# A graph layer on one core: W's first products in the chain from keys and values to the mix, and other places for the quads around it

## The chip, the cores and the metric

The kernel runs on one core of one Trainium2 chip. The metric is the device time of one execution in microseconds (us), lower is better. The core's engines each run their own instruction stream in order: PE (matrix products; PEld is its weight load), DVE (vector), ACT (scalar and activation), POOL (here it issues the row gathers and computes small powers), and SP (issues plain DMA transfers). They wait for each other through semaphores.

## The reference

The input is x, 12500 rows of 256 float32, and 200,000 edges sorted by destination. The layer adds three terms to x:

```python
xn = _layernorm(x)
support = xn @ W_gnn
agg = segment_sum(support[src] * edge_weight[:, None], dst, N)      # relu(agg) is added to x
k, v = layernorm per head of xn @ wk.T, xn @ wv.T                   # 4 heads of 64, with gains and biases
kv = einsum('bhsd,bhse->bhde', k, v) / S
mix = (q @ kv) @ wo.T + bo,  q = xn @ wq.T                          # added to x
x = x + ffn(_layernorm(x))
# ffn, 30 times: h += 0.01 tanh(h); h = silu(h); h = layernorm(h) * w + b; h = h @ W + bias
```

Since q, kv and wo act on xn one after the other, the whole attention term is xn times one 256 x 256 matrix. The kernel calls this matrix `mix`; it exists only when kv has been summed over all rows. Since W_gnn is linear, the kernel sums gathered rows of xn first and multiplies the sums by W afterwards.

## The kernel before

**Units.** Rows come in 98 tiles of 128; four tiles make a group (25 groups). Edges come in 1563 columns of 128. A gather (L182, an indirect DMA that POOL issues) fetches the 128 source rows of one column from xnd in DRAM. Four columns are a *quad* (391 of them), two quads an *octet*. `selections` builds on DVE the 0/1 and weight matrices of a quad (L208, L213) and, with the second quad, of its octet (L221). `sum_quad` (L234) multiplies four gathered tiles into the PSUM tile pq; `copy_quads` (L245, ACT) copies pq of a finished octet to sq; `add_quads` (L259) spreads it over 192 destination rows in the PSUM ring pa; `free_nodes` copies finished columns of pa to aT (L273, ACT) and clears them (L274, DVE). aT of a group is complete when its last octet is added; then W can be applied.

**Gathers.** Gather buffers are a ring of 16 (`ROWS`): a gather is issued only while `gathered < summed * 4 + 16`, so each `sum_quad` is followed by `gathers(4)`.

**Stages.** (1) Load and normalize x, write xnd, transpose xn into xnT, and the first 24 key tiles. (2) From tile 24 on, the loop at L793: per tile `KeyValue` (L288: xn times the key and value weights; L295 and L301 on ACT, L299, L305, L306 on DVE normalize it) and `kv_product` of the tile two before (L314, into pacc). A list `quad_at` says after which tiles a quad is summed; the quads' selections stand between the tile's two DVE halves. Also, small weight preparations (`rest`), whose inputs SP loads at the beginning of this stage. (3) The chain from keys and values to the mix: psum_kv (L823) is pacc copied; py (L828) = psum_kv times the key gains; y (L831) its copy; pbd (L835) = y times the value gains; bd (L838) its diagonal blocks; a product with wq (L846); `at` (L848 to L851) its centred copy; a product with wo (L855); mix (L860). Between its links stand five calls of `another_quad`. (4) The passes. `plan()` writes the order out beforehand with fixed costs: in each step one item, either "mix" of a group (L1009: xn times mix, then x is added, L1076), or "W" of a group (L1009: aT times W, L1080 adds a correction accw, L1081 applies relu and adds), or a "pass" of the 30 (transposes L996, product L1009, then ACT and DVE), and beside it quads, gathers and the start of a group. A group starts after its mix and W. At most five groups are in flight. An item's loads and transposes are issued in step k, its product in k + 1, what follows in k + 2. `accw` holds zeros, or another matrix of sums where a rare branch (L622) was taken; the register n_out chooses.

**Buffers.** The chain's PSUM tiles come from p_kv, three in rotation; the products of stage 4 from p_o, two in rotation; the loads of x and accw in stage 4 from two tiles xt, which reuse SBUF of the stages before, so that the first waits until the mix is done.

Of the kernel before, what the change touches and what calls it, by code (L numbers as in the profile page):

```python
# [8 lines left out]
F32 = mybir.dt.float32  # L9
# [7 lines left out]
P = 128  # L17
# [13 lines left out]
def gps_layer(  # L31
# [135 lines left out]
    class Edges:  # L167
# [2 lines left out]
        summed = 0  # L170
        added = 0
        freed = 0
        xg, sel, selq, sq, aT = {}, {}, {}, {}, {}
        pq = None

# [64 lines left out]
    def copy_quads():  # L240
        if ed.pq is not None and (ed.summed % 2 == 0 or ed.summed == NQ):
            o = (ed.summed - 1) // 2
            rows = min(Q, NE - o * O) * 2 * WIN
            sq = ge.tile([P, C], F32, name="sq")
            nc.scalar.copy(sq[:rows], ed.pq[:rows])  # L245
            ed.pq = None
            ed.sq[o] = (rows, sq)
# [18 lines left out]
    def free_nodes():  # L266
        while ed.freed < NS and last_of[ed.freed] < ed.added:
            j = ed.freed
            gi = j * SLOT // (G * P)
            if gi not in ed.aT:  # L270
                ed.aT[gi] = ge.tile([P, KC, G * P], F32, name="aT", bufs=3)
            c, d = (j % RING) * SLOT, j * SLOT % (G * P)
            nc.scalar.copy(ed.aT[gi][:, :, d : d + SLOT], pa[:, :, c : c + SLOT])  # L273
            nc.vector.memset(pa[:, :, c : c + SLOT], 0.0)  # L274
            ed.freed += 1
# [437 lines left out]
    with ExitStack() as ph:  # L713
# [14 lines left out]
        lk = w1.tile([D + 1, P // D, P], F32, name="lk")  # L728
        rv = w1.tile([D + 1, D], F32, name="rv")
        gcol = w1.tile([D, 2], F32, name="gcol")  # L730
        wo_nat = w1.tile([P, KC, C], F32, name="wo_nat")
        nc.sync.dma_start(out=wo_nat, in_=wo.rearrange("(k p) c -> p k c", p=P))
        f_nat = w1.tile([P, KC, C], F32, name="f_nat")
# [51 lines left out]

        quad_at, spent, n = {}, 0.0, 0
        for t in range(kv_done, NT + 2):
            quad_at[t] = spent > 7.0 + 5.2 * n
            n += quad_at[t]
            spent += 2.5 + (1.1 if quad_at[t] else 0.0)  # L790
        gathers(ROWS)
# [18 lines left out]
                sum_quad()  # L810
                gathers(Q)

        def another_quad():
            copy_quads()
            free_nodes()
            selections(1)
            add_quads()
            sum_quad()
            gathers(Q)


        psum_kv = w1.tile([D + 1, HEADS, D + 1], F32, name="psum_kv")
        nc.vector.tensor_copy(psum_kv, pacc)  # L823
        bd = w1.tile([P, KC, P], F32, name="bd")
        nc.vector.memset(bd, 0.0)
        py = p_kv.tile([D + 1, HEADS, P], F32, name="pkv")
        for hd in range(HEADS):
            nc.tensor.matmul(py[:, hd, :], lhsT=psum_kv[:, hd, :], rhs=lk[:, hd % (P // D), :], start=True, stop=True)  # L828
        another_quad()
        y = w1.tile([D + 1, HEADS, P], F32, name="y")  # L830
        nc.vector.tensor_copy(y, py)  # L831
        another_quad()
        pbd = p_kv.tile([P, HEADS, D], F32, name="pkv")
        for hd in range(HEADS):
            nc.tensor.matmul(pbd[:, hd, :], lhsT=y[:, hd, :], rhs=rv, start=True, stop=True)  # L835
        for hd in range(HEADS):
            r = slice(hd % (P // D) * D, (hd % (P // D) + 1) * D)
            nc.vector.tensor_scalar(bd[r, hd // (P // D), r], pbd[r, hd, :], 1.0 / N, None, ALU.mult)  # L838
        another_quad()


        at = w1.tile([P, KC, C], F32, name="at")
# [1 line left out]
        pm = p_kv.tile([P, KC, C], F32, name="pkv")  # L844
        for h in range(KC):
            nc.tensor.matmul(pm[:, h, :], lhsT=bd[:, h, :], rhs=wq_n[:, h, :], start=True, stop=True)  # L846
        another_quad()
        nc.vector.tensor_copy(at, pm)  # L848
        nc.vector.tensor_reduce(am, at, AX.X, ALU.add)
        nc.vector.tensor_scalar(am, am, 1.0 / C, None, ALU.mult)  # L850
        nc.vector.tensor_tensor(at, at, am[:, :, None].to_broadcast([P, KC, C]), ALU.subtract)  # L851
        pm = p_kv.tile([P, KC, C], F32, name="pkv")
        for m in range(KC):
            for h in range(KC):
# [1 line left out]
                    pm[:, m, :], lhsT=at[:, h, m * P : (m + 1) * P], rhs=woT[:, h, :],  # L856
                    start=(h == 0), stop=(h == KC - 1),
                )
        another_quad()
        nc.vector.scalar_tensor_tensor(  # L860
            mix, bo_r[:, None, :].to_broadcast([P, KC, C]), 1.0 / C, pm, op0=ALU.mult, op1=ALU.add
        )
# [8 lines left out]
    def plan():  # L871
        T_PASS, T_MATRIX, T_QUAD, T_GATHER, T_LAND, T_POW, T_STATS, T_CHAIN = 4.4, 3.5, 1.2, 1.25, 6.0, 1.3, 4.4, 14.0
        now, pool = 0.0, 4.0
        quads, got, started = ed.summed, ed.gathered, []
        whole, based = [], {}
        active, mixed, steps, k = {}, 0, [], 0
        landed = {t: 0.0 for t in range(got)}
        summed, passes = 0, 0
        pows = {}
        while len(based) < len(groups) or active or len(started) < len(groups):  # L880
            item, nq, cost, start = None, 0, 0.0, None
            octets = NO if quads == NQ else quads // 2
            while summed < len(groups) and octets > last_of[min((summed + 1) * G, NT) * P // SLOT - 1]:
                whole.append(summed)
                summed += 1
            ready = [g for g, (last, it, at) in active.items() if last + APART <= k and at <= now + 1.0]

            wanted = whole and mixed <= whole[0]
            if wanted or (not whole and not ready and mixed < len(groups)):
                item, cost = ("mix", mixed), T_MATRIX  # L890
                mixed += 1
            elif whole:
                item, cost = ("W", whole.pop(0)), T_MATRIX
                based[item[1]] = k
            elif ready:

                lead = 0 if len(started) == len(groups) else 1
                g = min(
                    ready, key=lambda g: (
                        active[g][1] + FFN_ITERS * (g // ABREAST) + lead * (g % ABREAST), active[g][0]  # L900
                    ),
                )
                it = active[g][1]
                passes += 1
                item, cost = ("pass", g, it), T_PASS
                if it == FFN_ITERS - 1:
                    del active[g]
                else:
                    active[g] = (k, it + 1, now + T_CHAIN)
                    pows[k + 2] = pows.get(k + 2, 0) + 1  # L910
            if (
                len(active) < ABREAST and len(started) in based and based[len(started)] + 3 <= k
                and (not started or k >= started[-1] + 4)
            ):
                start = len(started)
                started.append(k)
                active[start] = (k + 3, 0, now + 26.0)
                pows[k + 1] = pows.get(k + 1, 0) + 1
                pows[k + 5] = pows.get(k + 5, 0) + 1

            ng, pool = 0, max(pool, now)
            while got < min(NE, quads * Q + ROWS) and pool < now + (T_STATS - T_GATHER if pows.get(k) else max(cost, 1.0)):
                pool += T_GATHER
                landed[got] = pool + T_LAND
                got += 1
                ng += 1
            if pows.get(k):
                pool = max(pool, now + T_STATS) + T_POW * pows[k]
            ahead = 2 * G * P / STEP * (ABREAST + 0.2 + passes / FFN_ITERS)
            while quads < min(NQ, ahead) and nq < (1 if item else 2):  # L930
                if max(landed.get(t, 1e9) for t in range(quads * Q, min(NE, (quads + 1) * Q))) > now + cost:
                    break
                quads += 1
                nq += 1
                cost += T_QUAD
            steps.append((item, nq, start, ng))
            now += max(cost, 1.0)
            k += 1
        return steps
# [82 lines left out]
    for k in range(K + 3):  # L1022
# [40 lines left out]
        if kind2 == "pass" and not last:  # L1063
            act2(g2, pos.pop((kind2, g2)), s2)
        elif last:
            t0, nt = groups[g2]
            for q in range(nt // 2):
                h = pos[kind2, g2][:, q].rearrange("p c j -> p j c")
                r = slice(2 * q, 2 * q + 2)
                nc.vector.tensor_tensor(base[g2][:, r, :], h, base[g2][:, r, :], ALU.add)  # L1070
            pos.pop((kind2, g2))
            rows_io(out, base[g2], t0, nt, False, nc.sync)
            written[g2] = k
        elif kind2 == "mix":
            nt = groups[g2][1]
            nc.vector.tensor_tensor(base[g2], pos.pop((kind2, g2))[:, :nt, :], xts.pop((kind2, g2))[:, :nt, :], ALU.add)  # L1076
        elif kind2 == "W":
            nt = groups[g2][1]
            ac = xts.pop((kind2, g2))[:, :nt, :]
            nc.vector.tensor_tensor(ac, pos.pop((kind2, g2))[:, :nt, :], ac, ALU.add)  # L1080
            nc.vector.scalar_tensor_tensor(base[g2], ac, 0.0, base[g2], op0=ALU.max, op1=ALU.add)  # L1081
# [93 lines left out]
```

## Time and profile before

| | |
|---|---|
| median of 3 runs | 4166.28 us (4165.76 to 4167.11) |
| the profiled execution, its own time | 4167.84 us |
| its span, first to last instruction | 4166.0 us |
| gathers, L182 | 1563, 1594.1 us busy, 1020 ns each |
| products of the passes, L1009 po<-w,zT | 2668.0 us, 380 ns a record |
| quads, L234 | 264.6 us, 392 ns a record |
| key tiles, L288 | 196.5 us, 625 ns a record |
| mean TensorE clock granted | 0.997 |
| first matmul of py (L828), first mix product (L1009) | at 353.31, at 384.47 us |

Every float32 matmul leaves two records, so a quad has eight, a group's product sixteen. Busy times count from a record's start to its modelled end; a matmul that follows another overlaps it. In a timeline a row gives start, length, engine, line, what it writes from what, and in brackets the engine's idle time before it with what ended it. In a row of windows the busy time of PE, PEld, DVE, ACT and POOL follows the stretch and its length, each with the number of instructions, then the granted TensorE clock, the share of the DMA engines and GB/s.

### The profile page before, as it was taken

Reading aid. Unit: us, or ns where it says so; the run is one execution under the profiler, and the core shown is the slowest. Engines: PE = TensorE matmul, PEld = TensorE weight load, DVE = VectorE, ACT = ScalarE, POOL = GpSimd, SP = SyncE. Lnnn points to the kernel's source line nnn. Section 1 sums busy time; section 2 is a strip of 40 time slices with the busy share of each in tenths; the row PEclk is TensorE's granted clock in tenths of the full one; section 3 lists DMA queues with packets and bytes.
Section 4 is the critical chain, followed back from the end, with each engine's and each line's share of the span. In section 5 each row is a group of like instructions: output and inputs, shape, how many; then the busy total and the mean of one; then the engine's idle time right before and its main releaser. Section 6 shows DMA issues by size and latency. Waiting matters only on the chain.

```text
span 4166.0 us, 67989 instructions
## 1 busy us (share of the span) xinstructions
PE 4095.5 (98%) x24201; PEld 3346.7 (80%) x24201; DVE 3397.5 (82%) x7389; ACT 2544.1 (61%) x3762; POOL 2588.0 (62%) x3186
## 2 busy tenths in 40 slices
PE   8998999999999999999999999999999999999999
PEld 5555788888887888888788888888888888788888
DVE  8664788888888888888888888888888888888887
ACT  7431466666666666666666666656666666677776
POOL 3677777777776666666667667667667652222222
PEclk9999999999999999999999999999999999999999
DMA  8434422222222221112221221122222210000000
GB/s 258 120 106 138 142 80 65 77 75 72 71 83 73 60 63 56 56 56 60 89 65 57 67 63 59 54 75 77 66 64 58 65 44 14 16 1 1 1 1 23
DMA packets 147686, 278.35 MB, mean 67 GB/s; under 512 B 28047, under 2 KB 97197, under 8 KB 147341
## 3 DMA queue, kind: packets, MB, share of 16 engines
q0 software_dynamic: 75024, 204.97, 16.9%
q1 hardware_dynamic: 72173, 68.42, 5.3%
q8 instruction: 197, 3.23, 0.3%
q14 instruction: 148, 1.21, 0.1%
q10 hardware_dynamic: 144, 0.52, 0.0%
HBM read 247.68 MB, written 26.12 MB: 66 GB/s over the span
## 4 chain that ended last, share of the span: by engine, by line
PE 81%; DVE 10%; ACT 2%; issue 1%; POOL 1%; DMA 1%; POOLq 0%; ACTq 0%; DVEq 0%
PE po L1009 55%; PE pt L996 14%; PE pq L234 5%; DVE z L982 3%; PE pkv L288 3%; PE pa L259 3%; DVE st L968 2%; DVE s L961 2%; ACT s L955 2%; DMA xg<-xnd,src_i 1%; PE pacc L314 1%; POOL rs L974 1%; DVE f_st L1131 1%; DVE big L1070 0%; ACT s L962 0%
## 5 line engine op out<-in xcount | busy, mean ns | idle before, releaser
L1009 PE MATMUL po<-w,zT 128*128 128x256 f32 x11760 | 2668.0, 380 | 2.5 <-DVE big L1070 1.9
L1009 PEld LDWEIGHTS po<-w,zT 128*128 128x128 f32 x11760 | 2177.9, 190 | 279.6 <-issue 9.5
L182 POOL DMA_INDIRECT xg<-xnd,src_i x1563 | 1594.1, 1020 | 486.5 <-issue 333.3
L961 DVE SCALAR_TENSOR_TENSOR s<-s,po 128x1024 f32<-128x1024 f32 (+1 forms) x725 | 866.6, 1195 | 399.7 <-ACT s L955 398.6
L982 DVE TENSOR_SCALAR z<-s,st,rs 128x256 f32<-128x256 f32 x2940 | 1051.5, 420 | 77.7 <-POOL rs L974 73.8
L962 ACT ACTIVATE s<-s 128x1024 f32<-128x1024 f32 (+1 forms) x750 | 780.5, 1041 | 381.7 <-DVE s L961 376.0
L968 DVE BATCH_NORM_STATS2 st<-s 128x6 f32<-128x512 f32 x1470 | 937.0, 678 | 85.3 <-ACT s L962 85.3
L955 ACT ACTIVATE s<-po 128x1024 f32<-128x1024 f32 (+1 forms) x725 | 731.0, 1008 | 337.9 <-PE po L1009 337.6
L1003 ACT ACTIVATE zT<-pt 128x512 f32<-128x512 f32 x1470 | 800.6, 601 | 97.2 <-PE pt L996 96.4
L996 PEld LDWEIGHTS pt<-ident,z 128*128 128x128 f32 x5880 | 660.4, 142 | 195.6 <-issue 124.1
L996 PE MATMUL pt<-ident,z 128*128 128x128 f32 x5880 | 793.0, 276 | 20.9 <-DVE z L982 20.3
L974 POOL TENSOR_TENSOR rs<-ve,mhalf 128x4 f32<-128x4 f32 (+1 forms) x750 | 773.1, 1031 | 62.4
L972 POOL TENSOR_SCALAR ve<-st 128x4 f32<-128x4 f32 (+1 forms) x750 | 152.7, 204 | 939.6 <-DVE st L968 909.4
L234 PE MATMUL pq<-xg,sel 128*32 128x256 f32 x3126 | 264.6, 392 | 13.8 <-DMA xg<-xnd,src_i 13.8
L245 ACT COPY sq<-pq 128x256 f32<-128x256 f32 x196 | 72.3, 369 | 302.4 <-PE pq L234 302.3
L288 PE MATMUL pkv<-wkv,big 128*128 128x512 f32 x392 | 196.5, 625 | 7.1 <-DVEq L622 5.0
L259 PE MATMUL pa<-selq,sq 128*128 128x192 f32 (+2 forms) x1168 | 181.5, 291 | 1.0 <-ACT sq L245 1.0
L234 PEld LDWEIGHTS pq<-xg,sel 128*32 128x32 f32 x3126 | 65.4, 108 | 140.7 <-issue 114.5
L259 PEld LDWEIGHTS pa<-selq,sq 128*128 128x128 f32 x1168 | 169.5, 191 | 10.9 <-ACT sq L245 2.0
L273 ACT COPY aT<-pa 128x128 f32<-128x128 f32 x196 | 51.4, 262 | 203.7 <-PE pa L259 202.2
L288 PEld LDWEIGHTS pkv<-wkv,big 128*128 128x128 f32 x392 | 68.7, 195 | 73.7 <-issue 68.1
L295 ACT ACTIVATE sq<-pkv 128x512 f32<-128x512 f32 x98 | 58.2, 593 | 102.5 <-PE pkv L288 102.5
(150 smaller groups left out, 1523.8 us busy)
## 6 DMA issues: line engine op xcount, KB each, us to landing
xg<-xnd,src_i POOLq DMA_INDIRECT x1563
xt<-in_x_dram SPq DMA_DIRECT2D x48, 512.0 KB
xnd<-xt SPq DMA_DIRECT2D x24, 512.0 KB
xt<-accw SPq DMA_DIRECT2D x24, 512.0 KB
out_dram<-big SPq DMA_DIRECT2D x24, 512.0 KB
xg<-in_dst_dram SPq DMA_DIRECT2D x6, 128.0 KB
xg<-in_src_dram SPq DMA_DIRECT2D x6, 128.0 KB
xg<-in_edge_weight_dram SPq DMA_DIRECT2D x6, 128.0 KB
```

Of the source, the lines that this page charges most:

```text
L182: nc.gpsimd.indirect_dma_start(out=ed.xg[t], out_offset=None, in_=xnd, in_offset=bass.IndirectOffsetOnAxis(ap=src_i[:, t : t + 1], axis=0),)
L234: nc.tensor.matmul(ed.pq[j * 2 * WIN : (j + 1) * 2 * WIN, :], lhsT=sel[:, j, :], rhs=ed.xg.pop(q * Q + j), start=(q % 2 == 0), stop=last, ...
L259: nc.tensor.matmul(pa[:, k, c : c + hi - lo], lhsT=sq[:rows, k * P : (k + 1) * P], rhs=selq[:rows, lo - n0 : hi - n0], start=False, stop=( ...
L955: nc.scalar.activation(flat(s, nt), flat(h, nt), AF.Tanh)
L961: nc.vector.scalar_tensor_tensor(sf, sf, 0.01, flat(h, nt), op0=ALU.mult, op1=ALU.add)
L962: nc.scalar.activation(sf, sf, AF.Silu)
L968: nc.vector.bn_stats(st[:, q, :], s[:, q].rearrange("p c j -> p (c j)"))
L974: nc.gpsimd.tensor_tensor(rs[:, :nt], ve[:, :nt], mhalf[:, :nt], ALU.pow)
L982: nc.vector.tensor_scalar(z[:, j, :], s[:, j // 2, :, j % 2], sv[:, j, 1:2], rs[:, j : j + 1], ALU.subtract, ALU.mult)
L996: nc.tensor.transpose(pt[:, i, k, :], z[:, 2 * q + i, k * P : (k + 1) * P], ident)
L1003: nc.scalar.activation(zT[:, 2 * q : 2 * q + 2], pt, AF.Copy, bias=1.0)
L1009: nc.tensor.matmul(po[:, j // 2, :, j % 2] if paired else po[:, j, :], lhsT=lhsT(j, k), rhs=rhs[:, k, :], start=(k == 0 and (j % 2 == 0 or ...
```

## The change

Six edits act together.

- `quad_at`: no quad after the last nine key tiles (89 to 97); two quads come at their end (with tile 97 where the count so far is even, and at the step after). 40 quads are summed in the loop instead of 45.
- `another_quad` and its five calls go. Two quads are summed (`two_quads`) ahead of py and two ahead of mix, all with their selections built beforehand; at the start of stage 4, 44 quads are summed instead of 50.
- W's product of the first two groups is computed in the chain, two tiles at a time (`w_product`), and stored with accw added over aT itself (`w_stored`).
- The accw rows of these two groups are loaded at the beginning of stage 2 into two new tiles, ahead of wo_nat.
- The planner takes the mixes of these two groups first and gives them no "W" step; a group counts as based with its mix.
- The mix step of these groups applies relu to aT and adds it, in two halves (SCALAR_TENSOR_TENSOR on DVE).

The planner computes the rest of the order anew from 44 quads.

```diff
+        acs = [w1.tile([P, G, C], F32, name=f"ac{g}") for g in range(2)]
+        for g, (t0, nt) in enumerate(groups[:2]):
+            rows = accw[bass.ds(n_out * ((G + t0) * P), nt * P), :]
+            nc.sync.dma_start(out=acs[g], in_=rows.rearrange("(g p) c -> p g c", p=P))
         wo_nat = w1.tile([P, KC, C], F32, name="wo_nat")
...
-            quad_at[t] = spent > 7.0 + 5.2 * n
+            quad_at[t] = t == NT or (t == NT - 1 and n % 2 == 0) or (t < NT - 9 and spent > 7.0 + 5.2 * n)
...
-        def another_quad():
-            copy_quads()
-            free_nodes()
-            selections(1)
-            add_quads()
-            sum_quad()
-            gathers(Q)
+        def two_quads():
+            for _ in range(2):
+                sum_quad()
+                gathers(Q)
+        halves_of = lambda g, h: ed.aT[g].rearrange("p k (g n) -> p g k n", n=P)[:, 2 * h : 2 * h + 2]
+        def w_product(g, h):
+            assert ed.freed >= (g + 1) * G * P // SLOT
+            pw = p_kv.tile([P, 2, C], F32, name="pkv")
+            for j in range(2):
+                for k in range(KC):
+                    nc.tensor.matmul(
+                        pw[:, j, :], lhsT=ed.aT[g][:, k, (2 * h + j) * P : (2 * h + j + 1) * P], rhs=wg[:, k, :],
+                        start=(k == 0), stop=(k == KC - 1),
+                    )
+            return pw
+        def w_stored(g, h, pw):
+            nc.vector.tensor_tensor(
+                halves_of(g, h), pw.rearrange("p g (k n) -> p g k n", n=P),
+                acs[g][:, 2 * h : 2 * h + 2].rearrange("p g (k n) -> p g k n", n=P), ALU.add,
+            )
+        selections(ed.summed + 4 - ed.selected)
         psum_kv = w1.tile([D + 1, HEADS, D + 1], F32, name="psum_kv")
         nc.vector.tensor_copy(psum_kv, pacc)
         bd = w1.tile([P, KC, P], F32, name="bd")
         nc.vector.memset(bd, 0.0)
+        two_quads()
         py = p_kv.tile([D + 1, HEADS, P], F32, name="pkv")
...
-        another_quad()
         y = w1.tile([D + 1, HEADS, P], F32, name="y")
         nc.vector.tensor_copy(y, py)
-        another_quad()
+        copy_quads()
+        free_nodes()
+        pw = w_product(0, 0)
         pbd = p_kv.tile([P, HEADS, D], F32, name="pkv")
...
+        w_stored(0, 0, pw)
...
-        another_quad()
+        pw = w_product(0, 1)
+        add_quads()
+        w_stored(0, 1, pw)
...
-        another_quad()
         nc.vector.tensor_copy(at, pm)
...
         nc.vector.tensor_tensor(at, at, am[:, :, None].to_broadcast([P, KC, C]), ALU.subtract)
+        free_nodes()
+        for h in range(2):
+            w_stored(1, h, w_product(1, h))
+        ed.weighted = 2
         pm = p_kv.tile([P, KC, C], F32, name="pkv")
...
-        another_quad()
+        two_quads()
         nc.vector.scalar_tensor_tensor(
             mix, bo_r[:, None, :].to_broadcast([P, KC, C]), 1.0 / C, pm, op0=ALU.mult, op1=ALU.add
         )
...
-                whole.append(summed)
+                if summed >= ed.weighted:
+                    whole.append(summed)
...
-            wanted = whole and mixed <= whole[0]
+            wanted = mixed < ed.weighted or (whole and mixed <= whole[0])
             if wanted or (not whole and not ready and mixed < len(groups)):
                 item, cost = ("mix", mixed), T_MATRIX
+                if mixed < ed.weighted:
+                    based[mixed] = k
                 mixed += 1
...
             nc.vector.tensor_tensor(base[g2], pos.pop((kind2, g2))[:, :nt, :], xts.pop((kind2, g2))[:, :nt, :], ALU.add)
+            if g2 < ed.weighted:
+                aT = ed.aT.pop(g2).rearrange("p k (g n) -> p k g n", n=P)
+                for i in range(KC):
+                    bk = base[g2][:, :, i * P : (i + 1) * P]
+                    nc.vector.scalar_tensor_tensor(bk, aT[:, i], 0.0, bk, op0=ALU.max, op1=ALU.add)
```

More of the change, by code (lines that the diff above doesn't have):

```diff
@@ L172, in gps_layer @@
         freed = 0
+        weighted = 0
         xg, sel, selq, sq, aT = {}, {}, {}, {}, {}
```

## The prediction

> **What bounds the kernel now.** I first read the page's busy shares and its row of slices, then the PE's waits, then the windows around the step that the change touches, then the PE and POOL timelines there.
>
> ```profile
> PE 4095.5 (98%) x24201; PEld 3346.7 (80%) x24201; DVE 3397.5 (82%) x7389; ACT 2544.1 (61%) x3762; POOL 2588.0 (62%) x3186
> PE pq L234 <- DMA xg<-xnd,src_i: 13.6, 18, 1.9
> 296.00:343.00 47.00, 46.76 (x299) 25.63 (x301) 29.94 (x76) 16.09 (x40) 35.56 (x38) 1.00 0.36 106
> 349.00:384.00 35.00, 23.06 (x108) 10.96 (x108) 10.33 (x38) 2.18 (x7) 26.77 (x28) 0.98 0.45 135
> 382.40:384.50 2.10, 2.10 (x9) 0.72 (x9) 0.00 (x0) 0.00 (x0) 1.49 (x3) 0.50 0.37 123
> ```
>
> The first line (busy us per engine) says that TensorE (PE) is the bound: nothing helps that doesn't take PE work away or fill a hole in it. The second, from the PE's waits between 343 and 440 us, says where a hole is: 13.6 of the whole run's 13.8 us of waits for gathered rows fall there. The windows (us, then busy and count of PE, PEld, DVE, ACT, POOL, then granted clock) show it: key tiles fill PE (46.76 of 47), the chain from keys and values to the mix leaves 12 of 35 us open, with POOL at 26.77. The last window's clock is 0.50: after the holes PE even ran at half speed.
>
> ```profile
> 359.90 1.04 PE L234 MATMUL pq<-xg,sel 128*32 128x256 f32 x4
> 361.68 0.62 PE L234 MATMUL pq<-xg,sel 128*32 128x256 f32 x2 [0.73 <-DMA xg<-xnd,src_i]
> 362.94 0.62 PE L234 MATMUL pq<-xg,sel 128*32 128x256 f32 x2 [0.64 <-DMA xg<-xnd,src_i]
> 363.49 1.10 PE L835 MATMUL pkv<-rv,y 65*128 65x64 f32 x8
> ```
>
> In this PE timeline the quad (four gathers, eight matmul records) ahead of L835 is fed row by row. A whole quad takes 0.57 us where its rows are there; here it is stretched to 3.6. POOL issues a gather each 1.25 us, so a quad each 5.0 us, and PE runs in order: every link of the chain queues behind a quad that waits. The true hole is larger than the idle column, since a lone pair of matmuls counts 0.62 us busy but costs 0.14 in a stream.
>
> The true hole, from the start of key tile 89 (L288 at 319.10) to the first mix matmul (L1009 at 384.47), 65.4 us: key tiles 9 x (1.77 + 0.47) = 20.2; 13 quads x 0.57 = 7.4; seven octets' L259 at 0.7 to 0.95 = 5.6; the chain's own matmuls 1.02 + 1.0 + 1.0 + 1.92 = 4.9. Together 38 us of work, 27 us of hole.
>
> **The change, part by part.**
>
> *No quads in the last nine key tiles.* Six quads leave tiles 89 to 97 (two come back at the end). Key tiles can then follow each other at 2.24 us (L288 starts at 135.19 and 137.43, where there were no quads yet; DVE needs 2.05 of that per tile, so PE still sets it). Meanwhile POOL goes on. By 318.5 us it had issued 155 gathers; the ring lets it reach 168 = 38 x 4 + 16, at 318.5 + 13 x 1.25 = 335. It idles some 6 us until quad 38 frees its rows; that loses 5 gathers. But the four quads before L828's successor find all rows landed.
>
> *Two loads of accw (512 KB each) at the phase's start, on SP ahead of wo_nat and f_nat.* SP issues cost 0.4 each. Between 376 and 384.5 us two such loads ran beside gathers and a gather took 5.4 us to land instead of 2.8. Here the first quad is wanted at 139.76, its last gather is issued at 129.9: 6 us of cover after landing. f_nat is issued at 132.2 and first read at 148.8 (L753). Cost 0; if the cover failed, 0 to 3 us.
>
> *The chain.* I walk it from 322.10 (L288 of tile 90, unchanged until there), with the durations above:
> - tile 97 starts at 322.10 + 7 x 2.24 = 337.8. From its start to its L314 took 4.83 us (343.48 to 348.31); one selection now stands in DVE's round trip, +0.35: 343.0. The quads 38 and 39 (1.14) lie inside that wait.
> - L314 0.45, one octet 0.9, quads 40 and 41 1.14: 345.5. On DVE three selections (some 2 us) now stand ahead of the copy psum_kv, which ends at about 345.3: hidden, just. Without those quads it would cost up to 0.9.
> - py 1.02: 346.5. y comes 1.8 us after py's start, at 347.4; first half of W's product for group 0 (half of L1009's 3.56): 348.3, so y is covered.
> - pbd 1.0: 349.3. DVE then takes the sum (one 128x512 from PSUM, nearest row L860, 0.69) and the four bd pieces (0.94), to 350.4; PE has the second half 1.8 and an octet 0.9, to 352.0. Covered.
> - L846's successor 1.0: 353.0. DVE needs 3.6 from its start to `at` (368.48 to 371.99): 355.6; PE has group 1's product, 3.6, to 356.6. Covered.
> - the last product 1.92: 358.5; quads 42 and 43, whose rows were issued from 341 to 351 and land by 354, 1.14: 359.7; ACT's copy 0.55 (measured 0.52), octet 0.8, quad 0.57: the first mix matmul at **361.6**. mix itself is ready at 359.4.
>
> That is 384.47 - 361.6 = **22.9 us earlier**. Before mix, PE has done two W products more and six quads (three octets) less: left to do later is -2 x 3.6 + 6 x 0.57 + 3 x 0.84 = **-1.3**. With no hole PE keeps its clock; the first mix product took 4.36 against 3.72: **-0.65**.
>
> *The mix steps.* W's steps for groups 0 and 1 go; their mix steps get two half-size operations on DVE, nearest row L1081 (1.23 for twice the size, SBUF only). The sums moved into the chain cost 4 x 0.69. So DVE is even, and it is 82% busy.
>
> *What is late next.* After the first mix, POOL still gives a quad per 5.0 us while a step with mix and quad takes 4.1 plus half an octet, 4.6. With landings of 4.1 to 5.2 us (measured between 390 and 416) I find 0 to 0.9 us of wait in each of quads 45 to 50, 1.5 to 2.5 in all; before had 2.1 in the same place. The six owed quads also delay groups 3 and 4: by the changed order of instructions W of group 3 stands after 13 passes instead of 5. Some 12 steps more run with three groups in flight. Before's own such stretch (480 to 530 us) left 0.17 us open in ten steps; mixes fill it. I add **+1** for both. Far later the order on PE is the same again, so the 29 us left open after 600 stay.
>
> Sum: -22.9 - 1.3 - 0.65 + 1 = -23.9, taken as -24. The profiled execution's own time is 4167.84 (span 4166.0 and 1.8 around it), 1.6 above the median 4166.28: 4143.9 for it, **4142.5** for the median.
>
> **Two rules against the trace.** *Clock.* The Trainium skill, TensorE: Matmul & The Clock Gate, part "The HAM clock gate", says that PE falls to half clock after an idle window of about 3.4 us. The longest hole here is 1.93 us, so by the rule nothing would throttle and 1.7 us of my gain (2.10 x 0.5 + 4.3 x 0.15, the clock in the two windows from 382.4) would have no cause. The row shows 0.50 after a stretch that was merely thin (2.95 us busy of 6.4). The row decides; by the rule the sum would be -22. *Gather issue.* SBUF — State Buffer, "Who interferes with whom", infers that a two-input operation of DVE, such as tensor_tensor, doesn't hold up the writing of DMA descriptors. In the trace the gathers beside L1081 took 1.81, 1.78 and 1.80 us instead of 0.95, those beside L1080, with one input in PSUM, 0.95. By the rule the added operations cost POOL nothing; by the rows four halves cost what the two removed L1081 did, 1.7 us, and the chain's sums, which read PSUM, nothing. Even either way, unless each half meets a gather: +1.7 on POOL, of which the quad waits pass on a part.
>
> **Rivals.** *Half the gain.* The hole moves behind the first mix: POOL lost 5 gathers (6 us), and with slow landings each quad from 45 to about 66 waits 0.5 us: 11 us given back, 4154. For it: 5.0 against 4.6. Against: the planner leaves steps without a quad, and before had no such wait after 416 us. *Slower.* Three groups in flight don't cover a pass's own chain: products 3.5, ACT and DVE 1.0 + 1.2 + 1.0 + 1.3, POOL 1.2, normalizing 1.7, transposes 1.4, copies 1.2, some 13.5 us, against a round of four steps, 17 to 19 us. If DVE or POOL queue up, each of the 12 added steps leaves a hole; from 2.0 us a step the gain is gone, at 2.5 the time is 4142.5 + 30 = 4172. Against: 0.17 us in before's own stretch. *It doesn't do what it says:* the key tiles don't close up to 2.24 (ACT and DVE round trip), or y and bd aren't covered. At 2.6 a tile the loss is 2.5, with three links uncovered another 4: 4149; inside the range.
>
> **How the numbers follow.** The forecast's own range is 4136 to 4149, chance 0.73; half the gain (to 4158) 0.13; no change 0.03; slower 0.10; still more gain 0.01. 0.2% (8 us) is about what a measurement can tell from no change. Faster 0.87, same 0.03, slower 0.10. The range 4135 to 4154 takes in the forecast and the better half of the first rival, and leaves out some 0.2.
>
> **What would show it.** The first mix matmul at 360 to 363 us; L288 at 2.24 in tiles 90 to 97; PE's waits for xg between 340 and 420 from 13 to under 3; granted clock 1.00 throughout; after 600 us the same 29 us open. Wrong: waits of PE for xg spread over 365 to 500, or for z between 440 and 560.

## The result, and the profile after

| | before | after |
|---|---|---|
| median | 4166.69 us (4165.76 to 4167.15) | 4137.07 us (4136.03 to 4138.99, 4 runs) |
| the profiled execution, its own time | 4167.84 us | 4136.86 us |
| its span | 4166.0 us | 4135.1 us |
| first matmul of py, first mix product | at 353.31, at 384.47 us | at 345.12, at 360.54 us |

The ratio is 0.993, with a 95% interval of 0.9913 to 0.9947: 29.6 us faster. The forecast was 4142.5, its range 4135 to 4154. Lines have moved: L234 is now L235 (quads), L259 is L260, L288 is L289, L1009 is L1045; W's products in the chain are L833, py is L854, pbd L862, the products with wq and wo L876 and L888.

First the windows of after, of the same stretches as shown of before (us from the start, length, then busy time of PE, PEld, DVE, ACT, POOL, granted clock, DMA share, GB/s):

```profile
296.00:343.00 47.00, 46.26 (x294) 25.64 (x293) 31.86 (x78) 16.95 (x42) 32.36 (x35) 1.00 0.33 96
349.00:384.00 35.00, 34.31 (x199) 26.02 (x200) 18.60 (x50) 2.18 (x7) 26.57 (x28) 1.00 0.61 185
382.40:384.50 2.10, 2.10 (x14) 1.23 (x13) 0.00 (x0) 0.00 (x0) 1.56 (x2) 1.00 0.99 332
```

In the second row PE was busy 23.06 of 35 us before; now 34.31. In the third the granted clock was 0.50; now it is 1.00.

Then everything that PE waited for between 310 and 440 us (in total, times, longest):

```profile
PE pt L1032 <- DVE z L1018: 1.4, 1, 1.4
PE pa L260 <- ACT sq L246: 0.6, 1, 0.6
PE pacc L315 <- DVE kn L307: 0.5, 1, 0.5
PE pkv L854 <- DVE psum_kv L848: 0.3, 1, 0.3
PE pq L235 <- DVE sel L214: 0.2, 1, 0.2
```

The row of 13.6 us for gathered rows (xg) is gone; nothing of its kind took its place. And the walk that the prediction made by hand, as the PE timeline of after shows it:

```profile
321.58 1.88 PE L289 MATMUL pkv<-wkv,big 128*128 128x512 f32 x4
323.77 1.93 PE L289 MATMUL pkv<-wkv,big 128*128 128x512 f32 x4
326.01 1.94 PE L289 MATMUL pkv<-wkv,big 128*128 128x512 f32 x4
...
345.12 1.09 PE L854 MATMUL pkv<-lk,psum_kv 65*65 65x128 f32 x8 [0.34 <-DVE psum_kv L848]
346.04 1.89 PE L833 MATMUL pkv<-wg,aT 128*128 128x256 f32 x8
347.77 1.00 PE L862 MATMUL pkv<-rv,y 65*128 65x64 f32 x8
348.61 1.95 PE L833 MATMUL pkv<-wg,aT 128*128 128x256 f32 x8
350.39 1.05 PE L260 MATMUL pa<-selq,sq 128*128 128x64 f32 x8
351.29 1.03 PE L876 MATMUL pkv<-wq_n,bd 128*128 128x256 f32 x4
352.15 3.62 PE L833 MATMUL pkv<-wg,aT 128*128 128x256 f32 x16
355.61 1.89 PE L888 MATMUL pkv<-woT,at 128*128 128x256 f32 x8
357.43 1.07 PE L235 MATMUL pq<-xg,sel 128*32 128x256 f32 x16
359.12 0.92 PE L260 MATMUL pa<-selq,sq 128*128 128x192 f32 x4 [0.62 <-ACT sq L246]
359.97 0.64 PE L235 MATMUL pq<-xg,sel 128*32 128x256 f32 x8
360.54 1.78 PE L1045 MATMUL po<-mix,big 128*128 128x256 f32 x7
```

Key tiles follow at 2.2 us; between the links of the chain (L854, L862, L876, L888) stand W's products without a bracket, that is without a wait. The two brackets cost 0.34 and 0.62 us. The last row stops at the edge of this view; the whole first mix product takes 3.72 us.

**Where the 30.9 us of span came from.** The first mix product is 23.93 us earlier. What PE has to do after it I count from the order of instructions with one price for each kind (a pass 4.4 us, a quad 0.57, an octet 0.78, a product of mix or W 3.6; these prices are estimates from the timelines): 1.5 us less than before. Take this work and the start from the end of the run, and a remainder is left, which I call *left open*: waits, stretched instructions, half clock. It was 34.2 us before and is 28.6 after. 23.9 + 1.5 + 5.6 = 31.0. The same three numbers describe every experiment, each from one profiled execution:

| kernel | first mix product at | work after it, against before | left open |
|---|---|---|---|
| before | 384.47 | 0 | 34.2 |
| after | 360.54 | -1.5 | 28.6 |
| e1, quads kept in the last tiles | 377.09 | -5.3 | 33.8 |
| e2, no W products in the chain | 359.79 | +5.7 | 27.4 |
| e3, before with the rule of nine tiles | 363.74 | +5.2 | 32.5 |
| e4, six tiles | 363.46 | -3.4 | 32.8 |
| e5, eighteen tiles | 353.37 | +4.3 | 37.3 |
| e6, before with late groups | 384.64 | 0 | 33.3 |
| e7, after with later groups | 359.37 | -1.5 | 32.2 |

The first column holds some chance: e7 has the instructions of after up to the mix, and reaches it 1.17 us earlier, since its tile 90 starts that much earlier (320.42 instead of 321.58 us). From the start of tile 90 to the first mix product it takes 38.95 us and after 38.96; before takes 62.37 and e6, with the same chain, 62.55. So the chain itself is compared from tile 90, where it won 23.4 us.

### The profile page after: what moved, and what is told of

It is laid out like the page before. It is cut to its first block, busy times and chain, and to the rows that moved or that the text cites. A ratio compares the mean times of both kernels' runs of the same rounds, so it can differ in the third digit from the quotient of the medians.

```text
span 4135.1 us, 67992 instructions
## 1 busy us (share of the span) xinstructions
PE 4078.1 (99%) x24201; PEld 3342.6 (81%) x24201; DVE 3396.8 (82%) x7393; ACT 2545.3 (62%) x3762; POOL 2586.0 (63%) x3186
## 4 chain that ended last, share of the span: by engine, by line
PE 83%; DVE 9%; ACT 2%; issue 1%; POOL 1%; DMA 0%; POOLq 0%; ACTq 0%; DVEq 0%
PE po L1045 56%; PE pt L1032 15%; PE pq L235 5%; PE pkv L289 3%; PE pa L260 3%; DVE z L1018 3%; DVE s L997 2%; DVE st L1004 2%; ACT s L991 1%; PE pacc L315 1%; POOL rs L1010 1%; DVE f_st L1172 1%; DVE big L1106 0%; ACT s L998 0%; ACT big L1151 0%
## 5 line engine op out<-in xcount | busy, mean ns | idle before, releaser
L1045 PE MATMUL po<-w,zT 128*128 128x256 f32 x11760 | 2666.5, 380 | 1.6 <-DVE xt L1121 0.5
L1045 PEld LDWEIGHTS po<-w,zT 128*128 128x128 f32 x11760 | 2177.1, 190 | 278.7 <-issue 9.9
L235 PE MATMUL pq<-xg,sel 128*32 128x256 f32 x3126 | 251.6, 391 | 0.3 <-DVE sel L214 0.2
L289 PE MATMUL pkv<-wkv,big 128*128 128x512 f32 x392 | 196.6, 625 | 6.8 <-DVEq L623 4.6
L260 PE MATMUL pa<-selq,sq 128*128 128x192 f32 (+2 forms) x1168 | 181.2, 291 | 0.6 <-ACT sq L246 0.6
L260 PEld LDWEIGHTS pa<-selq,sq 128*128 128x128 f32 x1168 | 169.6, 191 | 10.3 <-ACT sq L246 1.3
L235 PEld LDWEIGHTS pq<-xg,sel 128*32 128x32 f32 x3126 | 62.5, 108 | 118.2 <-issue 113.1
L289 PEld LDWEIGHTS pkv<-wkv,big 128*128 128x128 f32 x392 | 68.8, 195 | 71.5 <-issue 66.2
```

Source lines behind the costliest of these rows:

```text
L235: nc.tensor.matmul(ed.pq[j * 2 * WIN : (j + 1) * 2 * WIN, :], lhsT=sel[:, j, :], rhs=ed.xg.pop(q * Q + j), start=(q % 2 == 0), stop=last, ...
L260: nc.tensor.matmul(pa[:, k, c : c + hi - lo], lhsT=sq[:rows, k * P : (k + 1) * P], rhs=selq[:rows, lo - n0 : hi - n0], start=False, stop=( ...
L1045: nc.tensor.matmul(po[:, j // 2, :, j % 2] if paired else po[:, j, :], lhsT=lhsT(j, k), rhs=rhs[:, k, :], start=(k == 0 and (j % 2 == 0 or ...
```

## The experiments

The theory at the outset (A) is the prediction's: rows come at one gather per 1.25 us and starve the chain; the rule for the last nine tiles lets them run ahead, and W's products fill the rest. What the rivals are is said where the expectations name them.

**Quads kept in the last tiles (e1).** The changed kernel, with W's products in the chain, but quads by the old rule; an even count at the end is kept.

```diff
-            quad_at[t] = t == NT or (t == NT - 1 and n % 2 == 0) or (t < NT - 9 and spent > 7.0 + 5.2 * n)
+            quad_at[t] = spent > 7.0 + 5.2 * n if t <= NT else n % 2 == 1
```

> The changed kernel with the old rule for quads in the last nine key tiles (44 in the loop, so that the count is even; then the same chain with W's products and two pairs of quads). Theory A (the hole was made by rows that hadn't arrived): the second quad of the first pair again waits for its rows, issued at 1.25 us each; py starts near 358.5 instead of 345.1, the first mix product near 374 instead of 360.5, with four quads more behind it (3.8 us of work): 4137.1 + 9.6, about 4146 to 4147. Theory B (the hole was the chain's own round trips between PE and DVE, which W's products cover): unchanged within 2 us, 4136 to 4139.

4157.17 us (4154.74 to 4158.77), ratio 0.9977 (0.9967 to 0.9986): 10.1 us under the kernel before in the same series of runs (4167.22), a third of the 29.6 us. PE's waits between 310 and 440 us have the row that the change had removed:

```profile
PE pq L235 <- DMA xg<-xnd,src_i: 4.7, 8, 0.8
```

The windows of e1 around it, and two rows of PE's timeline:

```profile
352.00:356.80 4.80, 2.42 (x8) 0.55 (x8) 0.00 (x0) 0.00 (x0) 3.67 (x4) 0.98 0.34 104
356.60:366.80 10.20, 10.20 (x34) 8.57 (x33) 2.43 (x7) 0.54 (x2) 7.77 (x9) 0.50 0.37 109
```

```profile
356.88 1.97 PE L854 MATMUL pkv<-lk,psum_kv 65*65 65x128 f32 x8
367.00 0.81 PE L260 MATMUL pa<-selq,sq 128*128 128x192 f32 x4
```

Rows feed PE one pair of matmuls at a time until 356.8 (busy 2.42 of 4.8 us), so py (L854) starts at 356.88, 11.8 us later than in after. Then PE is busy without a gap, but at half clock for ten us: from L854 to the octet (L260) behind the second W product takes 10.1 us, where after takes 5.3. 11.8 + 4.8 is the whole 16.6 us by which the mix is later (18.2 us if counted from tile 90, which starts 1.6 us earlier here than in after). I had expected 4146 to 4147, a miss: the waits for rows were in it, the half clock wasn't, nor the 5.2 us that the later stretch left open on top. This profiled execution is the fastest of the ten, 2.4 us under their median, so its row in the table says rather too little.

**No W products in the chain (e2).** The rule and the new places of the quads stay; W of the first two groups is a step of stage 4, like that of every other group.

```diff
-        pw = w_product(0, 0)
...
-        w_stored(0, 0, pw)
...
-        pw = w_product(0, 1)
...
-        w_stored(0, 1, pw)
...
-        for h in range(2):
-            w_stored(1, h, w_product(1, h))
-        ed.weighted = 2
```

> The changed kernel without W's products in the chain: both groups get their planned W step again, quads as changed. Theory A: PE idles in the chain's round trips, but the chain is the shorter for it: the first mix product at about 359 instead of 360.5, the two products (7.2 us) come later, and quads 44 and 45 wait some 1.5 us: 4143 to 4145, so most of the gain stays. Theory B: most of the gain goes, 4155 or more.

4142.98 us (4141.91 to 4143.3), ratio 0.9942 (0.9925 to 0.9958), a fraction under the expected 4143 to 4145. Three rows of PE's waits, then three windows of the links' stretch:

```profile
PE pkv L881 <- DVE at L876: 2.7, 1, 2.7
PE pq L235 <- DMA xg<-xnd,src_i: 1.1, 2, 0.9
PE pkv L861 <- DVE y L856: 0.8, 1, 0.8
```

```profile
343.90:347.40 3.50, 2.72 (x24) 2.48 (x23) 1.51 (x6) 0.20 (x2) 2.71 (x3) 1.00 0.38 102
347.50:357.70 10.20, 7.52 (x30) 4.18 (x28) 4.44 (x12) 0.27 (x1) 7.76 (x9) 0.50 0.35 100
349.50:352.10 2.60, 0.00 (x0) 0.00 (x0) 2.47 (x5) 0.00 (x0) 1.99 (x3) 0.50 0.37 101
```

The mix is 0.75 us earlier than in after, but tile 90, which no edit of e2 touches, had started 1.36 us earlier. From tile 90 the chain takes 39.57 us, 0.6 more than in after, although 7.2 us of products don't stand in it: it now waits for its own links and runs ten us at half clock, and the products are owed later. So in the chain they cost no time at all: they fill holes of DVE's round trips, and with them PE kept the full clock. They are worth 5.9 us (4142.98 - 4137.07), or 5.4 if each kernel is set against the kernel before of its own series (24.2 us of gain here, 29.6 with them).

**The rule of nine tiles alone (e3).** The kernel before, with the new `quad_at` line and nothing else.

```diff
-            quad_at[t] = spent > 7.0 + 5.2 * n
+            quad_at[t] = t == NT or (t == NT - 1 and n % 2 == 0) or (t < NT - 9 and spent > 7.0 + 5.2 * n)
```

> The kernel before with nothing but the new rule for the last nine key tiles; single quads between the chain's links as before, no W in the chain. Theory A: the first four of the chain's quads find their rows, the fifth waits (its rows can only be issued from 350 us): first mix product near 364.5, 7.2 us of W left for later: 4146 to 4149, about 19 of the 30 us. Theory B: 4160 or more.

4150.01 us (4149.26 to 4150.81), ratio 0.9958 (0.9941 to 0.9975), a little over the expected range: 17.2 us under the kernel before of the same series, by one line. The five calls in the chain still wait for rows, once for 2.94 us,

```profile
PE pq L234 <- DMA xg<-xnd,src_i: 6.9, 7, 2.9
```

and the clock is 0.72 between 362 and 368 us, under the first mix product (4.65 us instead of 3.72). From here to e2 it is 7.0 us, the worth of the quads' new places.

**Six tiles or eighteen (e4, e5).** In the changed kernel,

```diff
-            quad_at[t] = t == NT or (t == NT - 1 and n % 2 == 0) or (t < NT - 9 and spent > 7.0 + 5.2 * n)
+            quad_at[t] = t == NT or (t == NT - 1 and n % 2 == 0) or (t < NT - 6 and spent > 7.0 + 5.2 * n)
```

and the same with 18. Here the rival C said that the 4.6 us for which POOL idles cost something.

> The changed kernel with six key tiles free of quads instead of nine (42 quads in the loop, 46 at the start of the passes). POOL then never runs out of free gather buffers and loses no gather. Theory A, PE is the bound and two quads merely change their place: within 2 us of the changed kernel, 4135 to 4139. Rival C (POOL's 4.6 us of idle gathers are paid later in waits of PE): 4133 to 4134. If the last pair's rows were late after all: 4140.

> The changed kernel with eighteen key tiles free of quads (34 quads in the loop, 38 at the start of the passes); POOL idles some 15 us more, groups 2, 3 and 4 start later still (steps 17, 40 and 65 of the written order, instead of 11, 32 and 56). If only holes on PE count and the six quads merely move: the first mix product 5.8 us earlier, near 354.7, 5.8 us of quads more behind it, 4135 to 4139. If quads or late groups are paid for later: 4142 or more.

Six: 4141.74 (4140.84 to 4142.0), 4.7 us slower than nine, a miss. The mix comes 2.92 us later with only 1.9 us more work done in front of it, and rows are short, once ahead of the mix (0.46 us, at 327.6) and once behind it (1.34 us, at 379.5):

```profile
PE pq L235 <- DMA xg<-xnd,src_i: 1.8, 2, 1.3
PE po L1045 <- DVE big L1112: 1.1, 1, 1.1
```

So C falls: between 310 and 360 us POOL now never stands still for more than 0.3 us, and the kernel is slower all the same. When POOL stands still, the rows of the whole ring are issued, and this is what the chain lives on. The waits in these rows come to 2.9 us, of 5.2 to be explained (1.0 ahead of the mix, 4.2 left open behind it); the written order behind the mix differs too, so the rows aren't shown to be all of it. Eighteen: 4144.15 (4143.04 to 4144.9), 7.1 us slower than nine. The mix is 7.2 us earlier, but POOL stood 28.1 us before one gather; 5.8 us of work are put off, and the later stretch leaves 8.7 us more open. PE waits for no rows between 310 and 440 us here; 6.4 of the 8.7 us arise between 1024 and 1278 us, where the longest of PE's waits are two for z, 2.8 us together. So this early mix isn't kept; that the lost gathers are the reason is not shown.

**The later stretch (e6, e7).** The 5.6 us that after leaves open less were not in the prediction. About 3.0 of them arise by the time that group 3 gets its W, about 2.5 where the first five groups hand over to the next five (1235 to 1390 us). Theory D: groups 3 and 4 start later in after (the six owed quads), so that groups end at better distances. If so, the kernel before with late starts should gain, and after with still later ones too.

```diff
-                and (not started or k >= started[-1] + 4)
+                and (not started or k >= max(started[-1] + 4, {3: 32, 4: 56}.get(len(started), 0)))
```

for before (e6), and with 40 and 64 for after (e7).

> The kernel before with nothing changed but the planner's start of groups 3 and 4: not ahead of steps 32 and 56 of the written order (23 and 47 before), as in the changed kernel. Theory D (the part of the gain that the chain doesn't explain comes from the handing over between the first five groups and the next five, near 1240 to 1390 us, which is smoother when groups 3 and 4 lag more): the first mix product stays at 384.5, and the time falls by 2 to 3 us to 4164 to 4165. Rival: late groups cost, as the prediction had it (up to 1 us), or nothing: 4166 to 4168.

> The changed kernel with groups 3 and 4 held back further (steps 40 and 64 instead of 32 and 56). Theory D: another 1 to 3 us less at the handing over: 4134 to 4136. Rival: no less or more, 4137 to 4140.

4165.82 (4163.75 to 4167.07), ratio 0.9999 (0.999 to 1.0008), and 4140.07 (4139.23 to 4141.4), ratio 0.9937 (0.9923 to 0.995). Neither is what D expects: the handover (from W of group 9 to W of group 10) still leaves 6.4 and 5.8 us open (before 6.5, after 4.0). D falls. Over the other kernels the same stretch leaves 3.0 (e2), 4.0 (e5), 5.7 (e3, e4) and 7.1 us (e1), so no single edit sets it; what does stays open.

**Seven and twelve tiles, and the changed kernel again (e9 to e11, then e12 and e13).** Seven tiles (e9, e12) and twelve (e10) change the same line as e4:

```diff
-            quad_at[t] = t == NT or (t == NT - 1 and n % 2 == 0) or (t < NT - 9 and spent > 7.0 + 5.2 * n)
+            quad_at[t] = t == NT or (t == NT - 1 and n % 2 == 0) or (t < NT - 7 and spent > 7.0 + 5.2 * n)
```

Seven leaves PE's order as in after but for one quad, which goes from tile 97 back to tile 90: POOL would have more lead behind the mix, and the 1.7 us of stretched quads there might go (theory E). Twelve (`NT - 12`) was a point between nine and eighteen; e11 and e13 are the changed kernel itself.

> The changed kernel with seven key tiles free of quads. By the count this moves a single quad, from tile 97 to tile 90; everything behind is in the very order of the changed kernel (44 quads at the start of the passes). Its rows are there at tile 90, POOL gets four free buffers earlier and needn't idle, and DVE has one selection less ahead of the last key tile. Theory E (what the later stretch leaves open is set by the written order and by how many rows are ahead, not by chance of the run): the first mix product at 360.0 to 360.5, the 1.7 us by which quads 45, 48 and 49 were stretched go, the rest is as in the changed kernel: 1 to 2 us less than it, 4135 to 4136. If the later stretch is chance of the run: anywhere from 4132 to 4142.

> The changed kernel with twelve key tiles free of quads (two fewer in the loop, 42 at the start of the passes), so a new written order. First mix product 1.9 us earlier, 1.9 us of quads more behind it. Theory E: the chain is worth the same, and the later stretch takes a value of its own within what the kernels so far showed (27 to 37 us over the plain sum of the work, 28.6 in the changed kernel): 4136 to 4145, more likely above the changed kernel than below.

> The changed kernel itself, timed beside the two others on the same chip: 4136 to 4139, and a profile within 1 us of the first one at the first mix product and in what the later stretch leaves open (28.6 us).

> No quads in the last seven key tiles instead of nine, as in e9. Theory E (a quad moved from tile 97 back to tile 90 keeps all rows in front of the mix, and the stretched quads of the chain, 1.7 us, go): first mix product at 360.0 to 360.5, time 4135 to 4136, one or two us below the changed kernel in the same call. Rival (the later stretch gives it back, or the first mix product isn't earlier): the same as the changed kernel within 1 us, 4136 to 4139. If the instructions come late again, as in the call of e9 to e11 (the kernel before near 4240), only the difference to the changed kernel in this call is read.

> The changed kernel itself once more, beside the seven tiles. All theories expect 4136 to 4139 and a first mix product at 360.5, as in its own runs; near 4238 with waits that the trace puts down to nothing it shows, if the late instructions of the call of e9 to e11 belong to the chip and this is such a chip.

| | us | before, same series | ratio |
|---|---|---|---|
| e9, seven | 4227.06 (4223.44 to 4228.95) | 4241.03 | 0.9965 (0.9953 to 0.9977) |
| e10, twelve | 4236.78 | 4241.03 | 0.999 (0.9981 to 0.9999) |
| e11, changed | 4238.17 (4231.19 to 4241.44) | 4241.03 | 0.999 (0.9981 to 0.9999) |
| e12, seven | 4210.9 (4209.57 to 4222.67) | 4228.15 | 0.9959 (0.9946 to 0.9972) |
| e13, changed | 4220.17 (4218.11 to 4229.23) | 4228.15 | 0.9981 (0.9971 to 0.999) |

In both series (e9 to e11, then e12 and e13) the kernels took 60 to 100 us longer: the kernel before 74 and 61, the changed one 101 and 83. e12 and e13 ran on the chip on which e5 to e7 had run before, with the kernel before at 4166.24 then, so it isn't the chip as such. In these series engines stand still for nothing that the trace can name. DVE's timeline in e13:

```profile
395.94 0.41 DVE L848 COPY psum_kv<-pacc 65x260 f32<-65x260 f32 x1
396.36 0.27 DVE L850 MEMSET bd<- 128x256 f32 x1
414.45 0.69 DVE L856 COPY y<-pkv 65x512 f32<-65x512 f32 x1 [17.83 <-remote]
```

and the same wait in DVE's waits of e12:

```profile
DVE y L856 <- remote: 8.4, 1, 8.4
```

py, which y copies, ended at 397.5 in e13; DVE had nothing else to do, and began 17 us later. "remote" is what the profile says when a releaser is none of this core's known ones. In after this instruction waited 0.9 us, for py. Seven tiles is 11.1 and 9.3 us below the changed kernel in these series. This one wait differs by as much, 9.2 and 8.4 us with seven tiles (e9, e12), 18.0, 17.8 and 17.9 us with the others (e11, e13, e10), but it isn't shown to be the whole reason: of the profiled executions e9's is only 3.5 us shorter than e11's, and e12's 16.5 us shorter than e13's. So these runs say nothing on E: it would need a series without such waits. Seven tiles is the fastest kernel of these two series, and not shown to be so elsewhere. What holds the engines back stays open. Most of it stands ahead of the mix (in e13 the first mix product starts at 430.50 us, 70 of the 92 us by which this execution is longer than after's), and from 391.3 to 425.6 us in e13, around the long wait, the DMA queues moved gathered rows and nothing else, so no transfer of instructions ran there. The change's ratio, 0.993 where engines stand still only for what the trace names, shrinks to 0.998 and 0.999 there.

## Why the prediction was right

The time lies in the range, 5.4 us under the forecast; against the profiled execution's own time the gain was put 7.0 us too small (4143.9 forecast, 4136.86 measured). The mechanism is as predicted, for the chain; one term, that of the later stretch, was mis-sized. Had that stretch left as much open as before (5.6 us more), the profiled time would have been 4142.5.

- *The hole and its cause* (27 us of hole, fed by gathers): right. e1 gives the rows' wait back and loses two thirds of the gain.
- *Key tiles at 2.24*: right: 2.19 to 2.25 from tile 90 to tile 97, of which three starts are shown above. *POOL idles some 6 us*: 4.6 us, and e4, where it doesn't idle, is slower.
- *Loads of accw cost nothing*: right, as far as one start shows it: the first quad of the stage starts at 139.92 us instead of 139.76.
- *The chain, 39.5 us from tile 90*: it took 38.96, from a tile 90 that started 0.52 earlier, so the mix comes at 360.54, not 361.6. py's wait for psum_kv ("hidden, just") was 0.34; y, bd and at were ready before their products started, with 0.8, 1.5 and 0.9 us to spare.
- *Work owed, -1.3*: as counted, -1.5.
- *Half clock, -0.65*: right that it goes with the thin stretch. PE went to 0.50 in e1 after holes of at most 0.80 us, and in e2 at 347.5 us after holes of at most 0.78 us, with PE busy 2.72 of the 3.5 us ahead; the hole of 2.68 us came when the clock was already halved. The rule of the Trainium skill against which it was weighed (TensorE: Matmul & The Clock Gate, "The HAM clock gate": an idle window of about 3.4 us), read as a hole of that length, has neither. What I under-used is how much that costs: ten us at half clock in e1, on a PE that is busy. With both the W products and the landed rows PE kept its clock from tile 90 to the mix, in all four undisturbed traces (after, e4, e5, e7); with only one of them (e1, e2, e3) it lost it, so each protects the other's gain. How long the half clock lasts isn't fixed by the order of instructions (see the end).
- *What is late next, +1*: **the term that was wrong.** Quads 45, 48 and 49 are stretched to 1.18, 1.32 and 1.11 us instead of 0.64, 1.7 us together, inside the 1.5 to 2.5 that I gave; I set against them only before's 2.1 in the same place. Together with the clock term I had +0.35 for the later stretch; it came to -5.6. This part of the gain was not foreseen: that the forecast still holds is the width of the range, and that the surprise fell on the good side is luck, for other orders of the same work leave up to 8.7 us more open (e5). About 3.0 of that lies right behind the mix, where before waited 2.1 us for rows and ran its first mix product 0.65 longer; about 2.5 at the handover, which I had taken as equal because the order of instructions is equal behind it. PE's idle time after 600 us is indeed the same (28.95 us before, 28.74 after), so of the later part most sits in matmuls that the profile counts as busy. Why they are shorter stays open.
- *Half the gain* didn't come: no idle wait for rows between 340 and 420; POOL's lost gathers reached PE only in the 1.7 us of stretched quads, whose last rows came late. *Slower* didn't come: with three groups in flight PE stands idle for nothing at all between 440 and 600 us (busy 160.00 of 160 us).
- *POOL's price for DVE operations on SBUF*: the rows were right about the direction. POOL's timeline of after:

```profile
334.93 0.95 POOL L183 DMA_INDIRECT xg<-xnd,src_i  x1 [0.30 <-PE pkv L289]
340.46 0.94 POOL L183 DMA_INDIRECT xg<-xnd,src_i  x1 [4.58 <-PE pq L235]
...
350.45 0.95 POOL L183 DMA_INDIRECT xg<-xnd,src_i  x1 [0.30 <-issue]
...
354.21 1.31 POOL L183 DMA_INDIRECT xg<-xnd,src_i  x1 [0.30 <-PE pkv L833]
...
365.86 1.21 POOL L183 DMA_INDIRECT xg<-xnd,src_i  x1 [0.30 <-issue]
```

The second line is POOL's wait for quad 38. The gather at 350.45 runs beside a sum that reads PSUM (L840, 0.69 us) and takes its usual 0.95; the one at 354.21 beside a subtraction with both inputs in SBUF (L880, 0.69 us), and the one at 365.86 beside a half of the new mix step (L1117, 0.69 us): 0.36 and 0.26 us longer. Beside the next mix step's two halves (371.39 to 372.68) the gather at 372.37 took 1.13 and the one at 371.12, which had begun before them, its usual 0.95. So a half cost 0.2 to 0.3 us where it cost anything, against 0.83 to 0.86 beside the larger L1081 (1.78 to 1.81).

## What to carry to other kernels

When an in-order engine queues behind work that is fed from outside at a fixed rate, let the feed run ahead while the engine has other work, and put work whose inputs are already there between the links of a serial chain. How far ahead is a size to measure: six tiles and eighteen both lost over 4 us to nine. Count a thin stretch twice, once for its holes and once for the half clock that can follow it (ten us of it in e1 and e2). And compare two runs from the last point where their instructions are the same, not from the start: here that turned 0.75 us earlier into 0.6 us longer.

## What was not expected of the hardware

- Half clock came without a long hole (longest wait 0.80 us in e1, PE busy 2.42 of 4.8 us) and stayed for ten us of uninterrupted matmuls: from 356.6 to 366.8 us.
- It isn't the same in every execution of one order. Up to the mix e6 is the kernel before, which had half clock once in its chain, for some 3.4 us (from 382.4). e6 had it twice, for 3.3 and 6.7 us at the least, and still reached the mix only 0.17 us later:

```profile
358.90:362.20 3.30, 3.14 (x10) 1.51 (x10) 0.00 (x0) 0.37 (x2) 2.69 (x3) 0.50 0.40 114
379.40:386.10 6.70, 6.18 (x22) 3.68 (x23) 0.78 (x4) 0.64 (x2) 5.18 (x6) 0.50 0.69 227
```

- The same program took 4137 us in one series of runs and 4220 to 4238 in others, and single instructions started up to 18 us after their inputs were there. A rearrangement worth 30 us in the undisturbed series was worth 3 and 8 us in these.
